# Sixteen sublayers on one core: the order of work in four attention stages is rewritten

## Chip, cores and metric

The kernel runs on one core of a Trainium2 chip. Its metric is the device time of one run in microseconds (us). A core has five engines that matter here, each of which takes its instructions in order: PE (matrix products, with its weight loads listed as PEld), DVE (VectorE), ACT (ScalarE), POOL (GpSimd) and SP, which only issues transfers. PE writes its results to PSUM, which the kernel divides into eight banks of 128 partitions x 512 floats.

## The reference

The input x has the shape [16, 256, 128]: 16 sequences of 256 tokens with 128 channels. Sixteen sublayers follow, each `x = x + f(layernorm(x))`. Four of them are touched by the change, cut here to what is computed:

```python
def L1_attn_a(x):                      # "linear": 16 heads of 8
    q, k = elu(x @ Wq.T) + 1, elu(x @ Wk.T) + 1;  v = x @ Wv.T
    kv_state = einsum('bhnd,bhne->bhde', k, v);   k_state = k.sum(axis=2)
    attn = einsum('bhnd,bhde->bhne', q, kv_state) / max(einsum('bhnd,bhd->bhn', q, k_state), 1e-6)
    local = xp[:, :-2] * conv_w[:, 0] + xp[:, 1:-1] * conv_w[:, 1] + xp[:, 2:] * conv_w[:, 2] + conv_b
    return (attn + local) @ Wp.T + bp

def L1_ffn(x):                         # "experts": 8 experts, the best 2 of each token
    logits = einsum('nc,ec->ne', x, gate_w)
    top_vals, top_idx = top_k(logits, 2);         top_w = softmax(top_vals)
    act = silu(einsum('nc,ehc->enh', x, w1)) * einsum('nc,ehc->enh', x, w2)
    return einsum('ne,enc->nc', route(top_idx, top_w), einsum('enh,ech->enc', act, w3))

def L1_attn_b(x):                      # "decay": 16 heads of 8, every token sees every other
    q, k, v = x @ Wq.T + bq, x @ Wk.T + bk, x @ Wv.T + bv
    scores = einsum('bqhd,bkhd->bhqk', q, k) * 8 ** -0.5 * exp(-alpha * abs(i - j))
    return (softmax(scores) @ v) @ Wo.T + bo

def L2_attn_b(h):                      # "sinks": 16 heads of 64 for q, 4 for k and v
    x = rmsnorm(h);  q, k, v = rope(x @ Wq + bq), rope(x @ Wk + bk), x @ Wv + bv
    scores = where(abs(i - j) <= 128, q @ k, -1e9)
    probs = softmax(concat([scores, sinks]))[..., :-1]
    h = h + (probs @ v) @ Wo + bo
    return h + moe(rmsnorm(h))         # its own experts, not touched

def L3_attn_a(x):                      # "rope": 16 heads of 8, causal
    Q, K, V = rope(x @ Wq.T + bq), rope(x @ Wk.T + bk), x @ Wv.T + bv
    return softmax(where(causal, Q @ K * 8 ** -0.5, -1e10)) @ V @ Wo.T + bo
```

In the second `rope` the odd half of each pair is zero. The order of the sublayers is: an attention of layer 0, local, performer, local, **linear**, experts, **decay**, experts, causal linear, mix, **sinks**, mix, **rope**, adapters, a state-space layer, adapters.

## The kernel before

**Tiling.** The activations stay in SBUF, transposed: 128 channels on the partitions, 4096 tokens along the free dimension, in x and in two buffers of the same size, ha and hb. A stage is one sublayer. It walks over eight chunks of 512 tokens (two sequences each), and a chunk's work is cut into steps.

**Order.** The order of instructions is written by hand. A stage's loop runs over slots; in each it issues some step of several chunks, so that a chunk's next step comes a slot later, when its inputs are there. Each engine executes its instructions in exactly this order, so an instruction that has to wait holds up all that stand behind it on its engine. Helpers name the engine: `mm` (L504) and `tr` (L508) PE, `act` (L528) ACT, `tt` (L531), `ts` (L538, L540) and `stt` (L543) DVE, `gt` (L534) POOL. In the profile most instructions therefore carry the line of a helper, and one tells them apart by their tiles. PSUM banks are taken in turn from a group (`bank("s")`, `bank("o")`); a product that needs a bank waits until its last reader has emptied it.

**Normalization.** `centre_step` (L1759) subtracts the mean by a product, copies the result to dst and squares it: on POOL, from dst (tile nsq, the instruction L534 "nsq<-ha"), unless it is called with square=True, where ACT does it from the bank. `spread_step` (L1774) makes the inverse root, and a third step scales. A stage can lead the following one: `lead` (L1833) gives the steps that the next stage needs of a chunk as soon as its x is final.

**Routing and stores to the experts.** Where experts follow (after linear and after decay), the lead is the eight steps of `Sending.steps` (L3547): three of normalization, compare (L504's product with the gate, all pairs of logits compared on DVE, a mask multiplied on POOL: tile ahead), choose (ranks and the gates; the second gate and the token number are computed on POOL, into out), place (each token's row in its expert's list, idx), turn (the chunk transposed into out) and scatter. The last issues eight indirect DMAs from POOL (L3651, tile rows<-out,idx), each for 128 tokens, that write the rows of 130 floats to the experts' lists in DRAM. Eight chunks make 64 of them.

**linear (L1948).** `slots` (L1820) puts step i of chunk c into slot c + i: three of normalization, project (three products, q, k, v and the convolution l), sums, heads, join, out, and the eight of the routing. That is 16 steps, so 23 slots for eight chunks, and in the middle of the stage a slot holds eight steps of eight different chunks.

**small_stage (L2769)** is the loop of decay, causal linear and rope. Its unit is one pair of 128-token tiles (queries, keys) of one sequence, for all 16 heads; decay has four to a sequence, rope three. Slot n issues `score(n)`: four products into four of six "s" banks, with the exponentials to pt; what is due; and `weigh_by_head(n - 3)`: sixteen products of pt with the values, into an "o" bank. When a sequence's tile is done, it is copied to raw, a slot later `turn` transposes it and divides, and another slot later `join` transposes it back into ot; `out` follows in the same slot as the last join of a chunk: the product of ot and Wo, and the addition to x. The lead's steps follow out one slot apart. The stage's own steps are listed with the slot at which they come, counted from their chunk's first unit. In decay (L2908) two of these are on POOL: keys_by_edge (tile kx) and queries_by_edge (tile qx). In rope (L2981) `turned` makes the rotated q and k, `queries` the masked copies of q, `guard` two maxima on DVE that a later check of ranges uses.

**window_attention (L3117)**, the sinks stage, has four "s" and four "o" banks. Its unit is a pair of tiles for one side (8 of 16 query heads): slot n issues `score(n)` (two products, two exponentials), a slot later `masked` (a mask on DVE, and for the second key tile the sum of both units' exponentials on POOL: tile both), and `weigh(n - 4)`: eight products with v, or twelve with those for the denominator from both, and from there `inverse` (ACT) and `divide` (DVE, to ot). A side of a chunk has eight units. In six of its eight slots `prepare` issues the projections for the next side, one a slot: k, then q0 to q3 (`roped`, with the product with sin, t2, on POOL; `moved` a slot later does the rest on DVE and adds on POOL), and, once a chunk, V:

```python
for t in range(4):
    pv = self.bank("s")
    self.mm(pv[:, :T], n1[:, c * CH + t * P : c * CH + t * P + P], w["Wv"])
    v = p1.tile([P, T], F32, tag="v", name="v", bufs=8)
    self.tt(v, pv[:, :T], w["bv"], ALU.add)
```

`out` runs once a chunk with eight products from ot. `before` and `after` are the normalizations ahead of and behind the attention, both with their squares on POOL.

Of the kernel before, what the change touches and what calls it, by code (L numbers as in the profile page):

```python
# [14 lines left out]
ALU = mybir.AluOpType  # L15
# [1634 lines left out]
class Fast(Net):  # L1650
# [169 lines left out]
    def slots(self, n, *steps, last=()):  # L1820
# [3 lines left out]
        with self.tc.manual_schedule():  # L1824
            self.logs()
            for k in range(n + len(both) - 1):
                for i in (*reversed(range(len(steps))), *reversed(range(len(steps), len(both)))):
                    if 0 <= k - i < n and k < n + len(both) - 1:
                        both[i](k - i)
# [3 lines left out]
    def lead(self, pool, bank="ps", tables=False):  # L1833
# [3 lines left out]
        if self.following == "swiglu_moe":  # L1837
            return self.sending.steps(pool, bank)
# [109 lines left out]
    def linear(self, w):  # L1948
        x, h0 = self.x, self.ha
        nc = self.nc  # L1950
        with ExitStack() as st:
# [78 lines left out]
            self.slots(NCH, *norm, project, sums, heads, join, out, last=self.lead(p))  # L2030
# [738 lines left out]
    def small_stage(self, w, units, steps, tiles, evict, finish=None):  # L2769
# [7 lines left out]
        lag = 3  # L2777
        with ExitStack() as st:
            p = self.stage(st, "sm", 1)
            items = [(c, b, *u) for c in range(NCH) for b in range(2) for u in units]  # L2780
            pts, po, ots, os, later, due = {}, {}, {}, {}, [], {}
            lead = self.lead(p, "s")
            first = min(at for at, _ in steps) - 4
            steps = [(first + i, lambda c, i=i: self.norm_x_step(p, c, i, "s")) for i in range(3)] + list(steps)

            def score(n):
                c, b, it, jt, kind = items[n]
                k, q, _ = tiles(c, b, it, jt)
                pt = p.tile([P, 4, 4, P], F32, tag="pt", name="pt", bufs=4)
# [5 lines left out]
                rest = evict(kind, pt, ps)  # L2795
                if rest:
                    due.setdefault(n + 1, []).append((lambda _: rest(), None))
                pts[n] = pt

            def weigh(n):  # L2800
# [13 lines left out]
                if last:  # L2814
# [3 lines left out]
                    if b == 1:  # L2818
                        later.append(c)

            def weigh_by_head(n, slot):
# [13 lines left out]
                if last:  # L2835
                    raw = p.tile([P, CH], F32, tag="raw", name="raw", bufs=2)
                    self.copy_out(it, raw, po.pop(it))
                    due.setdefault(slot + 1, []).append((lambda n: turn(n, raw), n))
                    if it:
                        due.setdefault(slot + 2, []).append((join, n))  # L2840

            def turn(n, raw):
# [14 lines left out]
            def join(n):  # L2857
# [7 lines left out]
                if b == 1:  # L2865
                    later.append(c)

            def out(c):
# [5 lines left out]
                else:  # L2874
                    self.tt(x, x, pz, ALU.add)

            with self.share(s=6, o=2), self.tc.manual_schedule():
                self.logs()
                many = 2 * len(units)
                for n in range(first, len(items) + lag + (1 if finish else 3) + len(lead)):  # L2880
                    if 0 <= n < len(items):
                        score(n)
                    for f, c in due.pop(n, []):
                        f(c)
                    if later:
# [864 lines left out]
```

## Time and profile before

| | |
|---|---|
| runs (median of three) | 4494.93 us (4494.88, 4494.93, 4496.07) |
| the profiled execution | 4543.07 us |
| its span, first to last instruction | 4541.2 us |
| mean granted clock of PE | 0.94 |
| PE busy | 4018.9 us, 88% of the span |
| PE weight loads | 2165.2 us, 48% |
| DVE busy | 2572.4 us, 57% |
| ACT busy | 2364.5 us, 52% |
| POOL busy | 2164.6 us, 48% |
| instructions | 70868 |

The profile is one execution, recorded by the hardware; its span can be cut into stretches of time, and in this kernel a stretch is a stage:

| stage | us of the span |
|---|---|
| layer 0's attention | 0 to 128 |
| local, performer, local | 128 to 1926 |
| linear, with the routing for the experts | 1926 to 2103 |
| experts | 2103 to 2312 |
| decay, with the routing for the experts | 2312 to 2640 |
| experts | 2640 to 2834 |
| causal linear | 2834 to 2990 |
| mix | 2990 to 3040 |
| sinks | 3040 to 3600 |
| its experts, then mix | 3600 to 3915 |
| rope | 3915 to 4140 |
| adapters, state space, adapters | 4140 to 4541 |

How to read its lines: a busy PE is not PE at its peak, and the granted clock says at which share of its full speed the hardware let it run. "PE ps L504 <- DVE v L531: 37.6, 7, 5.4" in a list of waits means that PE's instruction of line 504, writing tile ps, waited seven times for a DVE instruction of line 531 on tile v, 37.6 us in all and 5.4 at most. A number in square brackets at the end of a timeline's line is the idle time of that engine before it and what ended it.

### The profile page before, as it was taken

Reading aid. Unit: us, or ns where it says so; the run is one execution under the profiler, and the core shown is the slowest. Engines: PE = TensorE matmul, PEld = TensorE weight load, DVE = VectorE, ACT = ScalarE, POOL = GpSimd, SP = SyncE. Lnnn points to the kernel's source line nnn. Section 1 sums busy time; section 2 is a strip of 40 time slices with the busy share of each in tenths; the row PEclk is TensorE's granted clock in tenths of the full one; section 3 lists DMA queues with packets and bytes.
Section 4 is the critical chain, followed back from the end, with each engine's and each line's share of the span. In section 5 each row is a group of like instructions: output and inputs, shape, how many; then the busy total and the mean of one; then the engine's idle time right before and its main releaser. Section 6 shows DMA issues by size and latency. Waiting matters only on the chain. (4 is left out here: it accounts for less than half of the span.)

```text
span 4541.2 us, 70868 instructions
## 1 busy us (share of the span) xinstructions
PE 4018.9 (88%) x27720; PEld 2165.2 (48%) x27720; DVE 2572.4 (57%) x4437; ACT 2364.5 (52%) x4489; POOL 2164.6 (48%) x1854
## 2 busy tenths in 40 slices
PE   7899999999899899974988779978999899898878
PEld 3455455475455355454854467532333343444333
DVE  4764665363566476372355533736776697476354
ACT  6665466445766366552356533545545454764432
POOL 4653454231655265235424344657878598321241
PEclk8999999999999999986999989998999899999979
DMA  1800000000000000004510054000000000000000
GB/s 56 322 1 1 10 2 1 18 1 1 19 1 1 3 2 1 1 18 129 169 38 16 16 174 151 1 32 1 1 1 1 3 1 9 6 1 17 6 0 20
DMA packets 70389, 142.30 MB, mean 31 GB/s; under 512 B 11006, under 2 KB 39300, under 8 KB 69920
## 3 DMA queue, kind: packets, MB, share of 16 engines
q1 hardware_dynamic: 57120, 114.46, 7.7%
q0 software_dynamic: 9568, 18.51, 1.2%
q8 instruction: 222, 3.64, 0.4%
q10 hardware_dynamic: 3360, 4.72, 0.3%
q14 instruction: 119, 0.97, 0.1%
HBM read 84.22 MB, written 55.25 MB: 31 GB/s over the span
## 5 line engine op out<-in xcount | busy, mean ns | idle before, releaser
L528 ACT ACTIVATE pt<-ps 128x512 f32<-128x512 f32 (+1 forms) x896 | 422.4, 538 | 450.3 <-PE ps L504 448.7
L504 PE MATMUL ps<-hb,w 128*128 128x512 f32 (+1 forms) x960 | 480.7, 630 | 8.1 <-DVE hb L543 5.1
L504 PE MATMUL ps<-w,hb 128*128 128x512 f32 (+2 forms) x896 | 414.6, 576 | 18.5 <-DVE t L531 10.9
L531 DVE TENSOR_TENSOR t<-ps,tab 128x512 f32<-128x512 f32 x512 | 319.5, 683 | 194.6 <-ACT sq L528 188.8
L534 POOL TENSOR_TENSOR t<-t,ss 128x1024 f32<-128x1024 f32 x128 | 243.7, 1904 | 306.0 <-ACT ss L528 196.7
L534 POOL TENSOR_TENSOR t<-t,t 128x512 f32<-128x512 f32 x256 | 320.6, 1274 | 13.3 <-PE ps L504 10.1
L504 PEld LDWEIGHTS ps<-hb,w 128*128 128x128 f32 (+1 forms) x960 | 180.8, 196 | 279.9 <-issue 225.7
L534 POOL TENSOR_TENSOR nsq<-ha 128x512 f32<-128x512 f32 x128 | 144.7, 1131 | 345.1 <-ACT ha L528 324.0
L504 PE MATMUL ps<-nsq,ct 128*128 128x512 f32 x368 | 219.2, 682 | 77.5 <-POOL nsq L534 59.2
L531 DVE TENSOR_TENSOR u<-u,ps 128x512 f32<-128x512 f32 x220 | 129.3, 592 | 228.9 <-PE ps L504 163.6
L528 ACT ACTIVATE pt<-pt 128x768 f32<-128x768 f32 (+1 forms) x160 | 170.1, 1063 | 154.3 <-DVE pt L531 154.3
L2184 POOL DMA_INDIRECT back<-y,x x156 | 152.7, 979 | 197.6 <-ACT y L528 171.3
L504 PE MATMUL ps<-ot,w 128*128 128x512 f32 x448 | 211.0, 607 | 26.9 <-ACT ot L528 19.9
L504 PE MATMUL ps<-qkt 64*128 64x192 f32 (+1 forms) x2048 | 216.2, 326 | 11.8 <-ACT pt L528 11.8
L504 PE MATMUL ps<-u,w 128*128 128x512 f32 (+1 forms) x448 | 218.2, 611 | 7.7 <-POOL u L534 7.7
L504 PE MATMUL ps<-xt,w 128*128 128x256 f32 x936 | 219.4, 385 | 4.4 <-DMA w<-in_moe_x 3.4
L504 PEld LDWEIGHTS ps<-qkt 64*128 64x128 f32 x2048 | 153.1, 188 | 134.9 <-ACT qkt L528 51.5
L528 ACT ACTIVATE nrs<-ps,ct 128x512 f32<-128x512 f32 x208 | 140.4, 686 | 147.9 <-PE ps L504 138.1
L504 PEld LDWEIGHTS ps<-w,hb 128*128 128x128 f32 x896 | 147.8, 193 | 143.1 <-issue 102.9
L531 DVE TENSOR_TENSOR ot<-ps,rd 128x512 f32<-128x512 f32 (+1 forms) x208 | 135.7, 653 | 135.9 <-ACT rd L528 106.7
L531 DVE TENSOR_TENSOR pt<-ps,w 128x384 f32<-128x384 f32 (+1 forms) x320 | 171.2, 576 | 73.1 <-PE ps L504 69.8
L528 ACT ACTIVATE u<-ps,w 128x512 f32<-128x512 f32 x160 | 106.9, 685 | 185.7 <-PE ps L504 183.1
(361 smaller groups left out, 9076.1 us busy)
## 6 DMA issues: line engine op xcount, KB each, us to landing
w<-in_moe_x SPq DMA_DIRECT2D x78, 533.0 KB
rows<-t SPq DMA_DIRECT2D x64, 520.0 KB
x<-rows SPq DMA_DIRECT2D x78, 130.0 KB
w<-in_local_f SPq DMA_DIRECT2D x8, 659.5 KB
y<-back SPq DMA_DIRECT2D x16, 256.0 KB
y<-back ACTq DMA_DIRECT2D x16, 256.0 KB
w<-in_local_f SPq DMA_DIRECT2D x4, 658.5 KB
back<-y,x POOLq DMA_INDIRECT x156
```

Source lines behind the costliest of these rows:

```text
L504: self.nc.tensor.matmul(out, lhsT, rhs, start=start, stop=stop)
L528: self.nc.scalar.activation(out, in_, func, **kw)
L531: self.nc.vector.tensor_tensor(out, a, b, op)
L534: self.nc.gpsimd.tensor_tensor(out, a, b, op)
L2184: nc.gpsimd.indirect_dma_start(views[2 * i + t], bass.IndirectOffsetOnAxis(ap=x[:, t, C : C + 1].bitcast(I32), axis=0), y[:, t], None, bou ...
```

## The change

Four things are rewritten; nothing else in the kernel differs.

- **Linear and routing.** `slots` takes `every`: step i of chunk c comes in slot c * every + i. Linear uses two. In the routing three POOL instructions of a chunk (the mask of ahead, the second gate, the token number) become DVE instructions.
- **Stores.** With `spread`, which small_stage asks for, the scatter step becomes four steps of two scatters, one slot apart. Only decay has experts behind it there.
- **small_stage.** `later` puts what is due into slots, and within a slot join comes ahead of turn and out. Out comes one slot after join instead of in the same. With `group=3`, which rope uses, three units are scored in three slots and weighed together in the third, three to five slots after their scores, and what would fall into a group's last two slots moves on. Rope's own steps move by a slot or so, and pt has six buffers instead of four.
- **Sinks.** Two units are weighed together in every odd slot; even slots prepare, with several projections in one step (k and q0; q1 and q2; q3 and half of V; half of V). V is made two tiles to a bank, with one addition of the bias for both. raw and t2 have four buffers. Out runs once for each side with four products. The squares of both normalizations are ACT instructions.

```diff
-            for k in range(n + len(both) - 1):
+            for k in range((n - 1) * every + len(both)):
                 for i in (*reversed(range(len(steps))), *reversed(range(len(steps), len(both)))):
-                    if 0 <= k - i < n and k < n + len(both) - 1:
-                        both[i](k - i)
+                    c, rest = divmod(k - i, every)
+                    if rest == 0 and 0 <= c < n:
+                        both[i](c)
...
-            self.slots(NCH, *norm, project, sums, heads, join, out, last=self.lead(p))
+            self.slots(NCH, *norm, project, sums, heads, join, out, last=self.lead(p), every=2)
...
+            def later(n, i, f, c):
+                for _ in range(i):
+                    n += 1 if group == 1 or n % group < group - 2 else group - n % group
+                due.setdefault(n, []).append((order.index(f) if f in order else 0, f, c))
...
-                pt = p.tile([P, 4, 4, P], F32, tag="pt", name="pt", bufs=4)
+                pt = p.tile([P, 4, 4, P], F32, tag="pt", name="pt", bufs=max(4, 2 * group))
...
-                    due.setdefault(slot + 1, []).append((lambda n: turn(n, raw), n))
+                    later(slot, 1, turn, (n, raw))
                     if it:
-                        due.setdefault(slot + 2, []).append((join, n))
+                        later(slot, 2, join, (slot, n))
...
                 if b == 1:
-                    later.append(c)
+                    later(slot, 3, out, (slot, c))
...
+                for i, f in enumerate(lead):
+                    later(slot, (2 if finish else 4) + i, f, c)
+            order = [None, join, turn, out]
...
-                    if lag <= n < len(items) + lag:
-                        weigh(n - lag) if finish else weigh_by_head(n - lag, n)
+                    if group == 1:
+                        mine = [n - 3]
+                    else:
+                        mine = range(n - 2 * group + 1, n - group + 1) if n % group == group - 1 else []
+                    for i in mine:
+                        if 0 <= i < len(items):
+                            weigh(i, n) if finish else weigh_by_head(i, n)
...
-                (0, lambda c: self.guard(ROPE, c, held[c, "q"], held[c, "k"])),
-                (-5, lambda c: turned(c, "q")), (-4, lambda c: turned(c, "k")), (-2, values),
-                (-3, lambda c: queries(c, 0)), (-1, lambda c: queries(c, 1)),
+                (-6, lambda c: turned(c, "q")), (-5, lambda c: turned(c, "k")), (-3, values), (-2, lambda c: queries(c, 0)),
+                (0, lambda c: queries(c, 1)), (1, lambda c: self.guard(ROPE, c, held[c, "q"], held[c, "k"])),
...
-            self.small_stage(w, units, steps, tiles, evict)
+            self.small_stage(w, units, steps, tiles, evict, group=3)
...
-                elif step < 5:
-                    g = step - 1
+                for g in ((0,), (1, 2), (3,), ())[step]:
                     roped("q", 4 * side + g, s, qs[i][:, g])
...
-                elif side == 0:
-                    for t in range(4):
-                        pv = self.bank("s")
-                        self.mm(pv[:, :T], n1[:, c * CH + t * P : c * CH + t * P + P], w["Wv"])
-                        v = p1.tile([P, T], F32, tag="v", name="v", bufs=8)
-                        self.tt(v, pv[:, :T], w["bv"], ALU.add)
-                        vs[c, t] = v
+                if side == 0 and step > 1:
+                    pv = self.bank("s")
+                    v = p1.tile([P, 2, T], F32, tag="v", name="v", bufs=4)
+                    for k in range(2):
+                        t = 2 * step - 4 + k
+                        self.mm(pv[:, k * T : k * T + T], n1[:, c * CH + t * P : c * CH + t * P + P], w["Wv"])
+                        vs[c, t] = v[:, k]
+                    self.tt(v, self.bt(pv), w["bv"][:, None, :].broadcast_to([P, 2, T]), ALU.add)
...
-                for g in range(8):
-                    self.mm(pz, w["Wof"][:, g * C : g * C + C], ot[:, g], start=g == 0, stop=g == 7)
-                self.stt(h[:, self.chunk(c)], pz, w["bo"], h[:, self.chunk(c)], ALU.add, ALU.add)
+                for g in range(4):
+                    at = (4 * side + g) * C
+                    self.mm(pz, w["Wof"][:, at : at + C], ot[:, g], start=g == 0, stop=g == 3)
+                hs = h[:, self.chunk(c)]
+                if side:
+                    self.tt(hs, hs, pz, ALU.add)
+                else:
+                    self.stt(hs, pz, w["bo"], hs, ALU.add, ALU.add)
...
-                    held["sq"] = self.centre_step(p1, self.x[:, s], h[:, s], "s")
+                    held["sq"] = self.centre_step(p1, self.x[:, s], h[:, s], "s", square=True)
...
-                    self.gt(held["sq"], h[:, s], h[:, s], ALU.mult)
+                    self.act(held["sq"], h[:, s], AF.Square)
...
-                    i, step = divmod(n + 8, 8)
-                    if step < 6 and 0 <= i < 2 * NCH:
-                        prepare(i, step, n)
-                    if lag <= n < len(units) + lag:
-                        weigh(n - lag, n)
-                    if n % 16 == 6 and n > 16:
-                        out(n // 16 - 1)
+                    if n % 2:
+                        for i in (n - 3, n - 2):
+                            if 0 <= i < len(units):
+                                weigh(i, n)
+                        continue
+                    i, step = divmod(n + 8, 8)
+                    if 0 <= i < 2 * NCH:
+                        prepare(i, step // 2, n)
+                    i, rest = divmod(n - 14, 8)
+                    if rest == 0 and 0 <= i < 2 * NCH:
+                        out(i)
...
-            net.gt(ahead.rearrange(flat), ahead.rearrange(flat), net.k["upper"][:, None, :].broadcast_to([P, 4, 64]), ALU.mult)
+            net.tt(ahead.rearrange(flat), ahead.rearrange(flat), net.k["upper"][:, None, :].broadcast_to([P, 4, 64]), ALU.mult)
...
-            net.gt(out[:, 1, :, C + 1], out[:, 0, :, C + 1], e, ALU.mult)
-            nc.gpsimd.tensor_scalar(
+            net.tt(out[:, 1, :, C + 1], out[:, 0, :, C + 1], e, ALU.mult)
+            nc.vector.tensor_scalar(
...
+        every = [(k, t) for k in range(2) for t in range(4)]
+        parts = [every[i : i + 2] for i in range(0, 8, 2)] if spread else [every]
+        return [norm(0), norm(1), norm(2), compare, choose, place, turn, *map(scatter, parts)]
```

## The prediction

> **What bounds the kernel now.** I read the busy time by stretches first, one stretch per stage, cut where a stage's own tiles begin and end (columns: stretch, its length, busy time and instructions of PE, PEld, DVE, ACT and POOL, granted clock, DMA share, GB/s). The four stages that the diff touches:
>
> ```profile
> 1926.00:2103.00 177.00, 97.92 (x546) 67.95 (x544) 96.77 (x304) 67.48 (x119) 80.39 (x102) 0.76 0.09 29
> 2312.00:2640.00 328.00, 255.28 (x3033) 139.71 (x3031) 180.58 (x458) 195.68 (x308) 124.18 (x118) 0.89 0.06 17
> 3040.00:3600.00 560.00, 496.89 (x3468) 182.37 (x3467) 377.77 (x511) 280.76 (x583) 429.05 (x242) 0.93 0.01 4
> 3915.00:4140.00 225.00, 199.44 (x2265) 105.87 (x2263) 163.59 (x221) 138.29 (x282) 52.54 (x31) 0.96 0.01 2
> ```
>
> They are linear attention with the routing that leads the first experts, decay attention with the same for the second, the sinks attention, and rope. PE sets the pace in all but linear, and in each the clock is below 1. So I looked for idle PE, stage by stage.
>
> *Linear*, the same view in stretches of 10 us, and its stores to the experts:
>
> ```profile
> 1976.00:1986.00 10.00, 10.00 (x54) 6.84 (x53) 9.01 (x20) 8.04 (x14) 0.00 (x0) 1.00 0.00 0
> 2006.00:2016.00 10.00, 7.29 (x46) 4.89 (x44) 9.31 (x38) 5.56 (x12) 3.91 (x7) 0.83 0.23 73
> 2046.00:2056.00 10.00, 1.33 (x12) 0.93 (x12) 4.09 (x20) 1.80 (x5) 7.99 (x10) 0.50 0.16 48
> 2086.00:2096.00 10.00, 0.00 (x0) 0.00 (x0) 0.00 (x0) 0.00 (x0) 7.68 (x8) 0.50 0.16 53
> ...
> L3651 POOL DMA_INDIRECT rows<-out,idx x64: 957/962/1347, 2014.5 to 2101.3; - x64
> ```
>
> To about 2010 PE and DVE are full; then POOL alone issues 64 scatters, 0.96 us each and 0.30 us between, and everybody waits for it. The stage ends when the last is out (2102).
>
> *Decay*, the timeline around one chunk's eight scatters (start, length, engine, line; in brackets the idle time before):
>
> ```profile
> 2466.11 1.12 PE L504 MATMUL ps<-x,ct 128*128 128x512 f32 x2
> ...
> 2472.31 0.60 ACT L528 ACTIVATE raw<-ps 128x512 f32<-128x512 f32 x1 [9.40 <-remote]
> 2472.81 0.90 ACT L528 ACTIVATE qz<-q,ct 128x256 f32<-128x256 f32 x2
> 2472.96 0.71 PEld L508 LDWEIGHTS ps<-ct,raw 128*128 128x128 f32 x4 [6.56 <-ACT raw L528]
> 2472.96 1.11 PE L508 MATMUL ps<-ct,raw 128*128 128x128 f32 x4 [5.73 <-ACT raw L528]
> ```
>
> ACT waits for a PE result whose matmuls are recorded as done at 2465.1, and what releases it is "remote": no instruction shown. This comes once per chunk, six times.
>
> *Sinks and rope*, what PE itself waits for in the steady part (total us, times, longest):
>
> ```profile
> PE ps L504 <- DVE v L531: 37.6, 7, 5.4
> ...
> PE ps L504 <- ACT ot L528: 11.7, 6, 2.1
> PE ps L504 <- POOL nsq L534: 3.2, 5, 0.7
> ```
>
> The first is sinks (3100 to 3550), the other two rope (3930 to 4110). After sinks' stall the granted clock is 0.50 from 3262.4 to 3269.2. Other DVE work delays v: PE has filled all four "s" banks with V, and the next score needs two of them back.
>
> And the price of a change of tile shape on PE, from sinks' timeline:
>
> ```profile
> 3291.74 1.13 PE L504 MATMUL ps<-q,k 64*128 64x512 f32 x4
> 3292.80 1.07 PE L3214 MATMUL ps<-pt,v 128*32 128x256 f32 x16
> 3293.80 7.13 PE L504 MATMUL ps<-ot,w 128*128 128x512 f32 x16
> 3300.86 1.13 PE L504 MATMUL ps<-q,k 64*128 64x512 f32 x4
> 3304.41 1.12 PE L504 MATMUL ps<-hb,w 128*128 128x512 f32 x2
> ```
>
> Sixteen passes in a row take 7.06 us to the next start, 0.44 each; the two of a lone hb,w take 1.06 (its neighbours follow at that distance), not 0.88. A change of shape costs 0.18 us.
>
> **Linear: chunks two slots apart.** A chunk has 16 steps, one a slot, and its scatter is the last (slot 15 for chunk 0 in both kernels). Before, slots 3 to 14 hold 77 steps (86 less 9 normalizations that the stage before has done) and last from 1934.5, the first projection, to 2014.5: 80 us, 1.04 us a step. With chunks two slots apart they hold 49: 51 us. A thin slot still costs its own chain (the first projection takes 5.8 us from its matmul to k), so I go slot by slot, 6 to 7.6 us for the odd ones with a projection and 1.5 to 4.5 for the even ones: 55 us. First scatter at 1990 instead of 2014.5. From there 64 x 1.27 = 81 us of issue; the first two chunks are 12 us apart and not 10.2, +4: end at 2075 instead of 2102, **-27 us**. Total slots rise from 23 to 30; the added ones lie under the scatters. Best: 1985 + 81 + 2, -34.
>
> Routing leaves POOL: 0.73 + 0.20 + 0.24 us a chunk. DVE gets it for 0.43 (its own 128x256 ahead) + 0.19 + 0.18 = 0.8 us; before the first scatter only one or two chunks of it count, later POOL is the bound. The six gaps where POOL did it between scatters (87.7 us for 81) are in the sum. A rule speaks against it: *SBUF — State Buffer*, Who interferes with whom, says that a DVE tensor_scalar or copy in a two-port mode locks GpSimd out for its whole length, and that GpSimd then can't write the descriptors of its DMAs. The row: 0.962 us median, 1.347 the slowest, though DVE works beside many. If every scatter took the slow row's length, 64 x 0.385 = 25 us come back and the gain is 2 us; by the row, 27. I take the row: small instructions of 0.2 us, and the trace already has such beside scatters.
>
> **Decay: two scatters a slot, out() one slot later.** The instructions are the same 64 scatters. POOL's queue has kx and qx behind them: kx starts when the eighth is issued (2470.7), but is needed some 11 us later, so it hides either way; two at a time put it behind 2.5 us. What the stall is worth: idle 3.2 + 4.6 + 5.7 + 5.7 + 5.8 + 5.4 = 30 us, and after each some 4.3 us of work at clock 0.50, six times 2.2 = 13: **43 us of the profiled execution**. Is it in the timed runs? The profiled execution took 4543.07 us, the median of the runs 4494.93: 48.1 apart. *Runtime: NRT & Kernel Launch*, The ~15µs preamble/postamble breakdown, puts a profile's own surplus at about 6.2 us for any kernel; *NOTIFIC — the notification-queue block*, Overflow, says that the path of the profiler's records pushes back on an engine rather than lose one. By both, 42 us are left to explain, and the stall is 43, where PE issues most instructions and the scatters run. By the row alone decay gains 43 us; by the rule the runs don't have the stall and gain nothing. I take the rule for the runs: **-3** (out's 0.47 us wait for ot goes, eight times, less a slot and three store slots at the end), ends +5 and -46. In the profiled time I expect -46.
>
> **Sinks: pairs, V in halves, squares on ACT, out per side.** V takes one bank for two tiles instead of four banks, and DVE empties it in one 512-wide instruction (0.68) instead of two (0.81). The wait for v should go: 5.35 us, and 6.3 us of work at half clock = 3.15, seven times: -60. Weighing two units together makes 4 changes of shape in two slots where there were about 6; merged ropings save some too: about 8 x 0.18 = 1.5 us a chunk, -12. Two nsq leave POOL (1.05 to 1.48 each) for 0.6 on ACT, which is half idle; out per side adds one DVE 0.69 a chunk. Against it: *both*, the sum of two tiles on POOL, was needed four slots after its score and is now needed two after. In a pair of slots PE has about 7.2 us; I followed the chain score, exp (1.1), mask (1.2 to 2.7), both (2.4 to 2.8) through POOL's queue, where two t (1.3 to 1.8) and two q adds (1.3 to 2.3) stand: it comes 2 to 4 us before PE needs it, the q3 add 3 us. POOL, 54.0 of 67.5 us now, would be at 51.5 of 57. Some of that slack will fail: I give back 12. **-60**, ends -75 and 0.
>
> **Rope: groups of three.** Weighing three units at once turns about 20 changes of shape a chunk into 12: 1.4 us. out() comes two slots after join, so the wait for ot (1.83 to 2.06) goes, nsq's 0.6 too, and in three of five chunks 3.4 us at half clock (1.7). That is 1.4 + 2.5 + 1.0 = 4.9 of some 29 us, six chunks: -29; a deeper start and end give back a little: **-25**, ends -35 and -5. The guard's two DVE 0.68 move a slot; DVE is 21 of 29 us busy. Causal shares small_stage with groups of one and keeps its order.
>
> **Sum.** -27 - 3 - 60 - 25 = -115. On the profiled time: 4543.07 - 115 - 43 = 4385; on the median: 4494.93 - 115 = **4380 us**. The profiled execution should come within some 6 us of the runs.
>
> **The rivals.** (1) *Decay's stall is in the runs too* and goes: "remote" is no proof of the profiler. Against it stands the 48 us. 4380 - 43 = 4337. Its opposite within decay, that two scatters a slot do nothing, is my own case. (2) *The shorter lag eats sinks' gain*: PE meets both or a q add about 1 us late in each of 64 pairs: 60 us back, 4440. For it: POOL at 90%, and its instructions stretch from 1.26 to 2.27 us beside DVE. (3) *Slower*: the same wait, in sinks' pairs, is the place; at 115 / 64 = 1.8 us a pair all is gone, at 2.5 us the kernel takes 4380 + 160 = 4540. It would need POOL 5 us later than I found, every pair. (4) *The scatters stretch* under DVE's new work: 25 us back, 4405; inside the range.
>
> **How the numbers follow.** My case 0.56 (own range 4355 to 4415, with rival 4 in it), stall in the runs 0.22, sinks' gain eaten 0.18, slower 0.04. Three medians within 1.2 us and 0.3% between executions make 0.2%, 9 us, the least that can be told. Faster 0.95, same 0.01 (the edge of the last two cases), slower 0.04. The range 4325 to 4440 holds nearly all of the first, most of the second and half of the third: 8 in 10.
>
> **What would show it.** Linear: the first scatter near 1990, 64 of them without DVE-made gaps, last near 2075. Decay: no "remote" wait; if one stays, the split doesn't cure it. Sinks: no PE wait for v, chunk period near 58 us, granted clock 1.0; wrong if PE waits for POOL both or q. Rope: chunks near 25 us, no wait for ot. The forecast is wrong if the profiled time stays 48 us above the runs, or if sinks keeps 560 us.

## The result and the profile after

The changed kernel takes **4424.94 us** (median of four runs, 4420.78 to 4430.12) against 4495.5 us: a ratio of 0.984, interval 0.9826 to 0.9861. It is 70.6 us faster; 115 were forecast. Its profiled execution took 4424.04 us with a span of 4422.3 us, so this time the profile and the runs agree.

The profile of before, which the prediction rests on, turned out to be a poor partner for that comparison: profiled a second time, the same kernel took 4497.84 us with a span of 4496.0. The 45 us between its two profiles lie almost wholly in decay (see the first experiment). All stages are therefore compared here between this second profile of before and the profile of after, both without the stall.

The view of stretches, one stretch per stage (columns: stretch, length, busy time and instructions of PE, PEld, DVE, ACT, POOL, granted clock, DMA share, GB/s), of the kernel before, second profile, in the order linear, decay, causal linear, sinks, rope:

```profile
1928.00:2105.00 177.00, 98.27 (x547) 68.07 (x545) 97.00 (x305) 67.45 (x119) 80.23 (x102) 0.76 0.09 28
2314.00:2597.00 283.00, 241.58 (x3037) 133.29 (x3035) 183.50 (x458) 195.38 (x309) 124.43 (x119) 0.95 0.06 19
2791.00:2947.00 156.00, 146.80 (x1622) 82.47 (x1621) 108.32 (x244) 75.89 (x152) 94.89 (x97) 0.99 0.02 8
2997.00:3556.00 559.00, 495.54 (x3468) 181.88 (x3467) 378.11 (x511) 280.57 (x583) 429.09 (x242) 0.94 0.01 4
3870.00:4095.00 225.00, 199.80 (x2266) 106.47 (x2264) 163.63 (x222) 138.45 (x282) 52.73 (x31) 0.96 0.01 2
```

The same of the kernel after:

```profile
1930.00:2087.00 157.00, 100.83 (x546) 67.79 (x544) 102.14 (x329) 67.70 (x119) 69.93 (x78) 0.82 0.10 32
2295.00:2609.00 314.00, 262.19 (x3036) 147.00 (x3034) 193.05 (x482) 196.91 (x309) 116.91 (x95) 0.90 0.06 18
2801.00:2961.00 160.00, 148.17 (x1620) 82.89 (x1621) 110.54 (x244) 75.49 (x152) 93.20 (x97) 0.99 0.02 8
3012.00:3512.00 500.00, 463.08 (x3468) 187.05 (x3467) 396.53 (x503) 280.51 (x598) 425.79 (x227) 0.98 0.01 4
3823.00:4021.00 198.00, 189.59 (x2267) 109.98 (x2265) 162.75 (x222) 140.04 (x282) 38.02 (x31) 0.99 0.01 3
```

Linear is 20 us shorter, **decay 31 longer**, causal linear 4 longer, sinks 59 shorter, rope 27 shorter: 71 in sum, which is what the runs show. Sinks and rope gained what was forecast. Where the forecast went wrong is decay, and it is a loss, not a smaller gain.

What stretched there is seen in the timeline of after around one routing step in decay:

```profile
2465.88 2.36 POOL L534 TENSOR_TENSOR qx<-qz,edge 128x1024 f32<-128x1024 f32 x1 [1.01 <-ACT qz L528]
2465.93 2.59 DVE L531 TENSOR_TENSOR ahead<-lg 128x256 f32<-128x256 f32 x1
...
2468.55 0.42 DVE L531 TENSOR_TENSOR ahead<-ahead,ct 128x256 f32<-128x256 f32 x1
...
2469.71 0.68 DVE L531 TENSOR_TENSOR ha<-ha,nrs 128x512 f32<-128x512 f32 x1
...
2470.54 1.95 PE L504 MATMUL ps<-ha,w 128*128 128x512 f32 x4 [1.10 <-DVE ha L531]
```

DVE's comparison of the logits starts 0.05 us after POOL's qx and ends just behind it: 2.59 us for an instruction that takes 0.42. The one after it, of the same size, takes 0.42 again. Behind both DVE scales ha, and PE waits 1.10 us for that. In the kernel before (second profile) the same place looks so:

```profile
2470.94 0.42 DVE L531 TENSOR_TENSOR ahead<-lg 128x256 f32<-128x256 f32 x1
...
2471.44 0.72 POOL L534 TENSOR_TENSOR ahead<-ahead,ct 128x256 f32<-128x256 f32 x1 [3.86 <-DVE ahead L531]
...
2475.80 0.18 DVE L3607 RECIPROCAL out<-g 128x4 f32<-128x4 f32 x1
...
2476.06 0.20 POOL L534 TENSOR_TENSOR out<-out,e 128x4 f32<-128x4 f32 x1 [3.89 <-PE ps L504]
...
2476.33 0.24 POOL L3609 TENSOR_SCALAR out<-ct 128x8 int32<-128x8 f32 x1
...
2476.65 2.38 POOL L534 TENSOR_TENSOR qx<-qz,edge 128x1024 f32<-128x1024 f32 x1
```

POOL's three routing instructions stood ahead of qx in POOL's queue. The first waited 3.86 us for DVE's comparison, and the second reads the reciprocal (out<-g) that DVE had ended 0.08 us before, whatever the profile puts its wait down to. So qx could not start before DVE was through with that part of the routing. Moved to DVE, these three no longer hold qx back, and it meets the comparison. What that costs is the question of the second experiment.

The Trainium skill has this meeting: *SBUF — State Buffer*, Who interferes with whom, says that a DVE instruction with two inputs in SBUF contends with a GpSimd instruction that reads SBUF; that the shared ports are an exclusive lock; and that the order of issue decides who blocks. This trace agrees: of the 2.59 us, 2.31 lie beside qx, and the instruction ends 0.28 us behind it, so at most 0.14 of its own 0.42 us got done meanwhile. One chunk earlier DVE's comparison came first, by 0.01 us (2428.32): it kept its 0.43, and qx took 2.64 us instead of 2.36. The prediction weighed the sentence of that section on scatters and overlooked this one.

### The profile page after: what moved, and what is told of

Same layout as the page of the kernel before. It is cut to its first block, busy times and chain, and to the rows that moved or that the text cites. A ratio compares the mean times of both kernels' runs of the same rounds, so it can differ in the third digit from the quotient of the medians.

```text
span 4422.3 us, 70823 instructions
## 1 busy us (share of the span) xinstructions
PE 3983.6 (90%) x27720; PEld 2180.9 (49%) x27720; DVE 2611.8 (59%) x4477; ACT 2365.8 (53%) x4505; POOL 2124.6 (48%) x1790
## 5 line engine op out<-in xcount | busy, mean ns | idle before, releaser
L504 PE MATMUL ps<-hb,w 128*128 128x512 f32 (+1 forms) x960 | 470.2, 624 | 6.3 <-issue 3.3
L534 POOL TENSOR_TENSOR nsq<-ha 128x512 f32<-128x512 f32 x112 | 122.4, 1094 | 310.7 <-ACT ha L528 298.6
L531 DVE TENSOR_TENSOR pt<-pt,w 128x1024 f32<-128x1024 f32 (+1 forms) x96 | 182.0, 1896 | 41.9 <-ACT pt L528 41.8
```

Source lines behind the costliest of these rows:

```text
L504: self.nc.tensor.matmul(out, lhsT, rhs, start=start, stop=stop)
L531: self.nc.vector.tensor_tensor(out, a, b, op)
L534: self.nc.gpsimd.tensor_tensor(out, a, b, op)
```

## The experiments

Three chips took part. On the first (b0, old_decay, decay_pool_routing, no_spread) before takes 4496.46 us, on the second (norm_early_pool and the experiments on linear, v_only) 4497.91, on the third (the other four) 4543.44.

### The kernel before, profiled again, and decay as it was

b0 is the kernel before without an edit. old_decay is the changed kernel with:

```diff
-            self.small_stage(w, units, steps, tiles, evict)
+            self.small_stage_old(w, units, steps, tiles, evict)
...
-            net.tt(ahead.rearrange(flat), ahead.rearrange(flat), net.k["upper"][:, None, :].broadcast_to([P, 4, 64]), ALU.mult)
+            (net.gt if pool_routing else net.tt)(ahead.rearrange(flat), ahead.rearrange(flat), net.k["upper"][:, None, :].broadcast_to([P, 4, 64]), ALU.mult)
```

Here small_stage_old is the loop of before, called from decay alone; pool_routing is true there, and the other two routing instructions choose by it in the same way.

> The kernel before, unchanged, profiled a second time. Theory P (decay's stall is made by the recording of the profile): the profiled execution is again some 43 to 48 us above the 4495 us of the runs, near 4541, with six 'remote' waits of ACT in decay. Theory R (the stall is a thing of the kernel, in every execution): the waits are there, and the profiled execution is within a few us of the runs. Third reading (the first profile was one odd execution): no 'remote' waits, and near 4495.

> The changed kernel with decay alone as it was: its old loop, one scatter step of eight, the three routing instructions on POOL there; the rest changed. Profile to profile decay became 14 us shorter by the change. Theory P: 43 us of that are the profiler's, so in the runs the change made decay 28 us longer, and this kernel takes 4425 - 28 = 4397 us, with a profiled execution near 4440 and the 'remote' waits back. Theory R: the stall is in the runs, and this kernel takes 4425 + 14 = 4439 us in both.

b0: 4497.84 us, amid the nine unprofiled runs of before on that chip (4493.03 to 4504.56), and no "remote" wait anywhere. So **profiling alone does not make the stall**; the third reading holds here, and the last experiments show where it comes back. old_decay: 4394.99 us, ratio 0.9774 (0.9761 to 0.9788), where the theory that the runs have no stall asked for 4397 and its rival for 4439; its profile (4393.84 us) has no "remote" wait either, which that theory had asked for. The change to decay costs the runs 30 us, and this kernel, without it, is faster than both.

### What in decay costs the 30 us

decay_pool_routing puts the three instructions back on POOL in decay, where spread is true, and keeps the new loop:

```diff
-            net.tt(ahead.rearrange(flat), ahead.rearrange(flat), net.k["upper"][:, None, :].broadcast_to([P, 4, 64]), ALU.mult)
+            (net.gt if spread else net.tt)(ahead.rearrange(flat), ahead.rearrange(flat), net.k["upper"][:, None, :].broadcast_to([P, 4, 64]), ALU.mult)
...
-            net.tt(out[:, 1, :, C + 1], out[:, 0, :, C + 1], e, ALU.mult)
-            nc.vector.tensor_scalar(
+            (net.gt if spread else net.tt)(out[:, 1, :, C + 1], out[:, 0, :, C + 1], e, ALU.mult)
+            (nc.gpsimd if spread else nc.vector).tensor_scalar(
```

no_spread sends all eight scatters in one step again:

```diff
-            lead = self.lead(p, "s", spread=True)
+            lead = self.lead(p, "s")
```

> The changed kernel with decay's three routing instructions on POOL again (linear keeps them on DVE). In the trace of the changed kernel one of DVE's two 128x256 instructions on tile ahead takes 1.9 to 2.6 us instead of 0.43 while POOL makes qx. Theory: this delays ha, the scores' multiplication and raw on DVE's queue and is most of what decay lost: PE's waits of 1.7 us for raw, 1.0 for ha and 0.4 for both, with the half clock behind them, 4.5 us a chunk in six chunks, go: 4400 us. Rival: DVE has room, and the lag of the stage's own steps is what costs: 4425, no difference.

> The changed kernel with decay's scatters in one step of eight, in the slot where the first two stood; nothing else. Theory P: in the runs eight at once cost nothing, 4425 within 6 us, and in the profile the 'remote' waits come back, some 40 us more than in the runs. Theory R: 43 us more in both, 4468. If POOL's queue matters (qx behind eight scatters): qx comes 8 x 1.27 = 10 us late in a chunk whose units are 4 us apart, and PE waits for qx by name.

decay_pool_routing: 4408.29 us, 0.9804 (0.9791 to 0.9817). The routing's place is worth 17 us. Tile ahead in its decay shows DVE's comparison at its own length again (first two rows), but now qx meets DVE's product on tile sel, which has two inputs in SBUF as well (last row):

```profile
L531 DVE TENSOR_TENSOR ahead<-lg x8: 424/425/426, 2356.7 to 2572.0; 128x256 f32<-128x256 f32 x8
L534 POOL TENSOR_TENSOR ahead<-ahead,ct x8: 725/733/736, 2357.2 to 2572.5; 128x256 f32<-128x256 f32 x8
L531 DVE TENSOR_TENSOR sel<-sel,at x8: 224/2297/2424, 2365.3 to 2576.1; 128x64 f32<-128x64 f32 x8
```

(minimum, median and maximum in ns; in after the first row reads 424/1909/2595 and the last 224/226/226, and in old_decay both are at their own length). Above its own length DVE loses 10.9 us on the two ahead instructions in after, and 12.7 us on sel here. So the 17 us can't be the time that DVE stands still: that did not shrink. What changed in the traces is what waits for DVE. First, the delayed comparison of after has ha behind it, for which PE waits 5.3 us in the middle of decay, and here 2.1. Second, the moved instructions stand in front of raw, which PE's transposition needs. Of after, then of decay_pool_routing:

```profile
2438.91 0.17 DVE L531 TENSOR_TENSOR out<-out,e 128x4 f32<-128x4 f32 x1
2438.99 0.17 DVE L3636 TENSOR_SCALAR out<-ct 128x8 int32<-128x8 f32 x1
2439.06 0.69 DVE L639 COPY raw<-ps 128x512 f32<-128x512 f32 x1
...
2439.89 0.63 PE L508 MATMUL ps<-ct,raw 128*128 128x128 f32 x4 [1.71 <-ACT pt L528]
```

```profile
2462.93 0.18 DVE L3634 RECIPROCAL out<-g 128x4 f32<-128x4 f32 x1
2463.02 0.66 DVE L639 COPY raw<-ps 128x512 f32<-128x512 f32 x1
...
2463.83 1.08 PE L508 MATMUL ps<-ct,raw 128*128 128x128 f32 x4 [1.42 <-DVE at L531]
```

PE starts 0.14 us after raw is done in both, whatever the profile names. Its wait is 1.71 us and not 1.42, in each of five chunks. In after, and the same in no_spread on this chip, all five waits are followed by 3.4 us at a granted clock of 0.50; here one of the five is, and in b0, where this wait is 1.31 us, none of six. At half clock 3.4 us of time hold 1.7 us of work, so by my estimate this makes some 8 of the 17 us (0.3 us five times, 1.7 four times), and the waits for ha 3. The two were not parted by a run, and the rest is not accounted for. no_spread: 4426.51 us, 0.9843 (0.9829 to 0.9856), without a "remote" wait: two scatters a slot do nothing on this chip, as the prediction's own case had it.

The other 13 us are the loop's. Decay's chunks, from one product of ot to the next, take 32.9 us in the middle of b0 and 34 to 35 in decay_pool_routing; the sum over the stage is 209.8 against 218.0, the first out comes 2.6 us later after the first score, and the last scatter 2.7 us later after the last out. norm_early_pool tests the one part of it that the prediction had not seen at all, the start of the normalization:

```diff
-            first = min(at for at, _ in steps) - 3 * group
+            first = min(at for at, _ in steps) - (4 if group == 1 else 3 * group)
```

> The changed kernel with the decay routing on POOL (4408 us) and, in decay and causal linear, the normalization one slot earlier, where it stood before. Theory N: the rewritten loop starts the normalization three slots ahead of the first step and not four; PE's waits for ha in decay, and POOL's square in front of ot in causal linear, come from that alone, and no other part of the new order costs anything. Then decay is where it was (4395) and causal linear gains its 4 us: 4391. Rival O: it is the new order of join, turn, out and lead: decay stays, causal gains 4, about 4404.

4403.08 us, 0.979 (0.9777 to 0.9803): the rival. Decay stays, and causal linear takes 156 us again instead of 160:

```profile
2783.00:2939.00 156.00, 146.81 (x1619) 82.47 (x1620) 108.30 (x244) 75.92 (x152) 94.52 (x97) 0.99 0.02 8
```

So causal's 4 us were the start of the normalization, a slot later. The reading that its square on POOL then stands ahead of ot in POOL's queue fits PE's waits for ot there (6.6 us in after, 3.5 in b0). For decay's 13 there was one suspect, sel's meeting with qx, which the old loop does not have. qx_later tried to part them, on the third chip:

```diff
-                (-2, lambda c: queries_by_edge(c, 0)), (0, lambda c: queries(c, 1)), (2, lambda c: queries_by_edge(c, 1)),
+                (-2, lambda c: queries_by_edge(c, 0)), (0, lambda c: queries(c, 1)), (3, lambda c: queries_by_edge(c, 1)),
```

> The kernel at 4403 us (decay routing on POOL, normalization early) with decay's second queries_by_edge one slot later, slot 3. In its trace DVE's product on tile sel, of 0.22 us, takes up to 2.4 us, beside POOL's qx, in seven of eight chunks, 12.7 us in all. Theory L (a DVE instruction with both inputs in SBUF stands still while POOL works): without that meeting decay's period goes from 34 to some 33 us, 4396. Rival: DVE has room there, 4403; what is left of decay's loss is the later out and lead at its ends, 5 us, and the period by something else.

It settles nothing. Tile sel in its decay:

```profile
L531 DVE TENSOR_TENSOR sel<-sel,at x8: 224/2298/2420, 2382.4 to 2609.9; 128x64 f32<-128x64 f32 x8
```

The product still takes 2.3 us instead of 0.22, in six of eight chunks as before, so the two still meet, and 4436.7 us (0.9764, 0.975 to 0.9777) on a chip where before takes 4543 can't be held against 4403 on another. In the middle of decay PE's waits come to 18 us in decay_pool_routing and 15 in b0, and its clock over the same stretches to 0.97 against 1.00: by my estimate from these some 10 of the 13 us. Which part of the new loop makes these waits stays open.

### Linear

linear_pool_routing is decay_pool_routing with the choice turned round, so that the routing is on POOL in linear alone:

```diff
-            net.tt(ahead.rearrange(flat), ahead.rearrange(flat), net.k["upper"][:, None, :].broadcast_to([P, 4, 64]), ALU.mult)
+            (net.gt if not spread else net.tt)(ahead.rearrange(flat), ahead.rearrange(flat), net.k["upper"][:, None, :].broadcast_to([P, 4, 64]), ALU.mult)
```

linear_every1 puts the chunks one slot apart again:

```diff
-            self.slots(NCH, *norm, project, sums, heads, join, out, last=self.lead(p), every=2)
+            self.slots(NCH, *norm, project, sums, heads, join, out, last=self.lead(p))
```

> The changed kernel with linear's routing instructions on POOL again (decay keeps them on DVE). By my sum the six gaps of the old scatter train, 6 us, are what the move is worth in linear: 4431. Rival: the DVE, full until the first scatter, pays back what POOL gains: 4425, no difference.

> The changed kernel with linear's chunks one slot apart again, routing on DVE. Profile to profile linear gained 19 us by the change. By my sum 6 of these are the routing's and the rest, 13, the earlier first scatter: 4438. Rival: the routing off POOL alone does it all, since POOL's 64 issues follow each other: 4425.

4451.33 us, ratio 0.99 (0.9884 to 0.9915), and 4437.71 us, 0.9872 (0.9857 to 0.9887). The second is as expected, the first is not. From the first projection to the last scatter's end linear takes 168.6 us in b0, 159.5 with the routing on DVE alone, **174.0 with the spacing alone**, and 147.4 with both: 9 us shorter, 5 longer, and 21 shorter. The spacing pays only with the routing off POOL. POOL's timeline with the spacing alone shows why:

```profile
2008.05 0.96 POOL L3678 DMA_INDIRECT rows<-out,idx  x1 [0.30 <-issue]
2009.02 0.75 POOL L534 TENSOR_TENSOR ahead<-ahead,ct 128x256 f32<-128x256 f32 x1
2012.60 0.56 POOL L534 TENSOR_TENSOR out<-out,e 128x4 f32<-128x4 f32 x1 [2.83 <-DVE out L3634]
2013.22 0.24 POOL L3636 TENSOR_SCALAR out<-ct 128x8 int32<-128x8 f32 x1
...
2013.78 1.05 POOL L3678 DMA_INDIRECT rows<-out,idx  x1 [0.15 <-POOL v L1976]
```

The mask waits behind eight scatters, DVE's choice waits for the mask, and POOL's gate waits 2.83 us for DVE before the next eight may start: 5.7 us from the start of a chunk's last scatter to the start of the next one's first, six times, where two scatters of one chunk are 1.3 apart. In b0, with the chunks one slot apart, this step was 2.5 us at most.

### Sinks: is it V's banks?

v_only edits the kernel before, and only V in it:

```diff
-                    for t in range(4):
-                        pv = self.bank("s")
-                        self.mm(pv[:, :T], n1[:, c * CH + t * P : c * CH + t * P + P], w["Wv"])
-                        v = p1.tile([P, T], F32, tag="v", name="v", bufs=8)
-                        self.tt(v, pv[:, :T], w["bv"], ALU.add)
+                    for u in range(2):
+                        pv = self.bank("s")
+                        v = p1.tile([P, 2, T], F32, tag="v", name="v", bufs=4)
+                        for k in range(2):
+                            t = 2 * u + k
+                            self.mm(pv[:, k * T : k * T + T], n1[:, c * CH + t * P : c * CH + t * P + P], w["Wv"])
+                            vs[c, t] = v[:, k]
+                        self.tt(v, self.bt(pv), w["bv"][:, None, :].broadcast_to([P, 2, T]), ALU.add)
```

v_one_step edits the changed kernel, so that both halves of V fall into one step:

```diff
-                if side == 0 and step > 1:
+                for u in range(2) if side == 0 and step == 3 else ():
...
-                        t = 2 * step - 4 + k
+                        t = 2 * u + k
```

> The kernel before with one change in sinks: V goes two tiles to a bank, in the same slot, and one 512-wide addition of the bias takes the place of two of 256. By my step the wait for v, 5.35 us and the half clock behind it seven times, is worth 60 us, and all else in sinks cancels: 4496 - 60 = 4436. Rival: the wait only moves to the next thing that is late in the slot, and pairs and merged steps are what gains: 4480 or more.

> The changed kernel with all of V in one step of sinks (two banks, in the last even slot) instead of a half in each of two. In the kernel before, the two-bank V alone took only 12 us off, and PE still waited 3.6 us for v, whose addition came 6 us after its product, behind seven instructions of DVE. Theory D: what removes the wait is that each half asks one bank of a DVE that is less far behind; then some 3.6 us and 1.7 for the half clock come back in seven chunks: 4462. Rival: the pairs leave DVE room by then, and two banks in one slot do no harm: 4425.

v_only: 4486.09 us, 0.9976 (0.9966 to 0.9986). That is 12 us and not 60. PE's waits in the steady part of sinks, of v_only and then of after (total us, times, longest):

```profile
PE ps L504 <- DVE v L531: 25.2, 7, 3.7
```

```profile
PE ps L3232 <- POOL both L534: 9.6, 14, 1.6
PE ps L504 <- POOL q L534: 7.2, 13, 1.0
```

In the trace of v_only DVE takes up the addition for V some 6 us after PE has made it, behind a normalization (2.21), a peak that waits for POOL's q, a division, a rotation and a shuffle. In b0 PE waits for v before the very next score (5.37 us at 3220.80); with two banks left free one more score gets through, and PE waits 3.58 before the one after. So what is late is DVE, and more free banks only put the wait off. v_one_step (4453.2 us, 0.9803, interval 0.9789 to 0.9816) ran on the third chip, so its sinks stage is read alone:

```profile
3035.00:3538.00 503.00, 462.73 (x3469) 187.20 (x3468) 404.46 (x503) 279.31 (x598) 420.06 (x227) 0.98 0.01 4
```

503 us against 500 in after (both_old_loops, below, has 501 for the changed sinks on the same chip), and no wait for v: the rival. V in halves is worth 2 or 3 us. The rest, some 45 us, is left for the other edits of sinks together. That the order in pairs makes most of it, since an odd slot has 40 passes of weighing for PE and no new projection for DVE, is likely and not shown: which part counts (the pairs, the wider steps, out per side, the squares) was not tried apart.

### Rope, and a version below both

rope_group1 weighs rope's units one by one:

```diff
-            self.small_stage(w, units, steps, tiles, evict, group=3)
+            self.small_stage(w, units, steps, tiles, evict)
```

both_old_loops is old_decay with causal linear, too, in the loop of before:

```diff
-            self.small_stage(w, [(0, 0, 0), (1, 1, 0)], steps, tiles, evict, finish)
+            self.small_stage_old(w, [(0, 0, 0), (1, 1, 0)], steps, tiles, evict, finish)
```

> The changed kernel with rope's units weighed one by one again (group of one), the rest of the new loop and rope's new slots kept. Profile to profile rope gained 27.6 us. By my sum the grouping itself is worth the 1.4 us of tile shapes in each of six chunks, and out's own slot the waits for ot: 4425 + 8 = 4433. Rival: out one slot after join is not enough with groups of one, the wait for ot stays, and the group makes the whole gain: 4452.

> The changed kernel with decay and causal linear both in the loop of before (decay with one scatter step and its routing on POOL); linear, sinks and rope stay changed. Decay's old loop alone gave 4395; causal linear's 4 us were given back by the earlier normalization in another run (4408 to 4403): 4391, below both kernels. If causal's loss depends on what decay does, 4395.

Both ran on the third chip, where before takes 4543.44 us (4540.95 to 4549.63): 4458.49 us, ratio 0.9814 (0.9801 to 0.9828), and 4450.84 us, 0.9796 (0.9783 to 0.981). Neither expected time holds, since they were counted for another chip; the stages can be read. Rope in rope_group1 takes 202 us against 198 in after and 225 before, and PE's waits for ot are down to 0.5 us:

```profile
3854.00:4056.00 202.00, 192.45 (x2263) 104.43 (x2261) 163.31 (x221) 140.23 (x282) 32.89 (x32) 0.99 0.01 2
```

So the grouping makes some 4 us, read across two chips, and what rope_group1 keeps makes 23: out's own slot, join ahead of turn, and rope's moved steps, not parted further. The sum had 8 and 21. And causal linear in both_old_loops takes 156 us. Its decay is the surprise:

```profile
2308.00:2637.00 329.00, 257.37 (x3030) 140.12 (x3030) 180.27 (x457) 194.53 (x308) 122.30 (x116) 0.89 0.06 19
...
2466.30 0.60 ACT L528 ACTIVATE raw<-ps 128x512 f32<-128x512 f32 x1 [9.32 <-remote]
```

329 us for the loop that takes 284 in old_decay, with the "remote" waits of the first profile. Here the unprofiled runs (4448.29 to 4455.39) are as long as the profiled one (4449.53), so they must have them too. The changed decay takes 329 on this chip, too (in rope_group1), 15 more than in after, but with such waits at one moment only (of DVE and ACT, 6.8 and 5.7 us) and not in six chunks. So **the stall goes with a chip, not with profiling**: there the old decay loses 45 us and the new one 15, and the two come out even. Whether it is the two scatters a slot that spare the new one was not tried: no_spread ran where there is no stall.

## Why the prediction was right and wrong

The time fell inside the range, and the sign was right; the likeliest time, 4380, was 45 us too low. That the range holds it is luck: it lies above the own case's 4415, in the part that was left for a loss in sinks, and the loss came in decay. By its steps:

| step | forecast | measured | |
|---|---|---|---|
| linear | -27 | -20 | 55 us to the first scatter were 62 |
| decay, runs | -3 | +31 | the step that failed: the routing there was put at nothing |
| causal linear | 0 | +4 | the start of the normalization was overlooked |
| sinks | -60 | -59 | right in size; not by V's banks |
| rope | -25 | -27 | right; the grouping gave 4, not 8 |

**Decay.** "The instructions are the same 64 scatters" is the step that failed. The routing's three instructions move in decay, too, and the sum counted them in linear alone, by their own length of 0.8 us. On DVE they cost 17 us there. POOL's qx, which they had held back, meets DVE's comparison, with ha behind it; and their own 0.3 us in front of raw lengthen a wait of PE from 1.42 to 1.71 us, after which the clock falls in five chunks and not in one. Both are in the traces, no run parts them, and DVE stands still as long with the routing back on POOL. The loop's new order costs the other 13, and which part of it is open.

**The stall.** That the runs behind the median did not have it was right, and with it the forecast that splitting the scatters brings them nothing. The reason given, that the profiler's records push back on the engine, is refuted: b0's profile has no stall, and on another chip the unprofiled runs are as long as with it. So the forecast about the runs was right by luck. The 48 us between profile and median look like a difference between chips: the first profile's 4543.07 us and six waits are those of the third chip, though which chip made it is not on record. The profiled time was missed, too (4385 against 4424.04), and the agreement of profile and runs "within some 6 us" came for another reason. The Trainium skill (*Runtime: NRT & Kernel Launch*, The ~15µs preamble/postamble breakdown) has a profile's total time about 6.2 us above the reported one; no such surplus shows in b0 or after, whose profiled executions lie among their runs.

**Linear.** The train of scatters was right: 64 in 85.3 us against 85, with medians of 0.967 us beside more DVE work, so the rule that would have cost 25 us did not bite. The thin slots before it were mis-sized, by 7 us. The split, 6 for the routing and 21 for the spacing, was wrong: the routing alone gains 9, and the spacing alone loses 5.

**Sinks.** The wait for v went, the clock rose from 0.94 to 0.98 and a chunk takes 59.4 us instead of 67.7. But the step named the banks, and v_only shows them to be worth 12. POOL's both and q came late by 17 us in all, more than the 12 given back and far from the rival that needed 60. That the total came out at -59 all the same is in part luck, since the term for the banks was wrong by most of its size and the pairs' by as much the other way.

**Causal** does not keep its order, as the prediction had it: the new loop's `first` starts the normalization three slots ahead and not four for groups of one.

## What to carry to other kernels

Before taking a slow instruction off a busy engine, look at what stands behind it in that engine's queue: the instruction may be holding that back, and what is released can land on the engine that just took over the work. Then ask what stands behind the place where it lands: here DVE stood still about as long with the routing on either engine, and by the traces 0.3 us in front of raw were enough to bring PE a half clock. Price an edit in each stage that uses the code, not only in the one it was written for. And before explaining a gap between a profile and the runs, profile the same kernel once more on another chip.

## What was not expected of the hardware

- A wait of PE of 1.71 us was followed by 3.4 us at clock 0.50 five times of five (after), one of 1.42 us once of five (decay_pool_routing), one of 1.31 us never of six (b0).
- A DVE tensor_tensor with both inputs in SBUF stands still while POOL works from SBUF: 2.59 us for 0.42 beside a qx of 2.36, 2.30 for 0.22 (sel), where DVE's products with one input in PSUM (pt<-ps,dec, 128 of them in that stage) keep 0.68 to 0.69 throughout.
- On one of three chips ACT takes up a product of PE about 7 us after PE is recorded as done with it, behind eight scatters of POOL, once a chunk (2459.17 to 2466.30 in both_old_loops): before takes 4540.95 to 4549.63 us there and 4492.84 to 4504.56 on the two others. The changed linear is longer there as well: its 64 scatters take 98.3 us in rope_group1 against 85.3 in after, and DVE waits for "remote" among them, 10.5 us at most. What makes that chip do so is open.
